# A four-layer graph network on one core: the last layer's messages with 384 radial columns and a second accumulator chunk, its frames made one layer earlier

## The chip, the core and the metric

The kernel runs on one core of a Trainium2 chip, as one program. The metric is the device time of one execution in microseconds. The kernel before takes 22,061.15 us, the median of 3 runs (22,058.3 to 22,079.04).

## The reference, cut to what matters

There are 12,500 nodes with 32 features each and 400,000 edges, sorted by target. Four layers follow each other; each sums messages over the edges into their targets, adds the result to `x` and applies a layernorm. Only the last layer's messages are changed. The 32 features are 8 scalars (kind l=0) and 8 vectors (l=1).

```python
R = relu(abs_distances[:, None] @ w1 + b1) @ w2 + b2     # 64 hidden, 384 radial values an edge
Y = spherical_harmonics(rel_vec)                         # the edge's direction
Fj = features[src]
...
# for each pair (lo, li) of output and input kinds, and each lf between |lo-li| and lo+li:
acc = acc + _NORM[i] * einsum('euv,ef,evi,ofi->euo', Rb[..., k], Yf, Fb, C)
...
out = zeros.at[dst].add(msg)
x = _layernorm(x + out)
```

If the vectors are turned into a frame of three orthogonal directions that goes with the edge (one of them along the edge), the tensor C becomes sparse: each output component (8 scalars; 8 vectors along each of three directions) is a sum over 16 inputs, weighted by radial values. That makes 32 sums of 16 products an edge. The two directions across the edge share one set of radial weights, so there are three different sets of 8 x 16 for the four kinds of output.

Layer 2 uses `edge_attr_2` to make three Gaussian weights an edge, and sums the products of these with `x[src]`.

## The kernel before, in words

**Tiling.** Edges stand 128 to a column. A step handles T = 5 columns (640 edges), a turn is G = 25 steps, a layer has NG = 25 turns, 625 steps in all. At every turn, `prepare` makes what depends on the edges alone for 25 steps (L924 for layer 2, L988 for layer 3). It is called for the next turn in the middle of the present one (`turns`, in `edge_pass`).

**A step.** GpSimd gathers the source rows with five indirect DMAs into `xg` (L338). A one-hot matrix `hot` says which of 64 nodes of a window each edge goes to; layer 3 loads it from DRAM, where layer 0 left it. TensorE multiplies the messages by it, five columns into one PSUM tile `agg` (L368), and VectorE adds `agg` into the accumulator `acc` in SBUF, at a column that a register holds (L388). Features lie on the partitions of `acc`, nodes along it.

**Layer 2** copies five steps' gathered rows into PSUM by ScalarE (L396), from a ring of three batches, makes 96 products and a count, and accumulates 97 rows. Its `prepare2` computes the Gaussians: four VectorE instructions (L930 to L944) and an exponential on ScalarE. In turn 1 it also zeroes layer 3's accumulator (L926).

**Layer 3** is made in four parts, which `run_ahead` (L403 to L428) puts in an order by hand: the products of step s, then the front and radial part of step s+1, then the reduction of step s, then the addition and the aggregation.

- `front3` (L1030): SP loads the distances into `dist` (L1037), ScalarE makes `h` (L1042); VectorE multiplies the gathered vectors by the three frame directions (`tv`, L1056, three instructions) and sums them (L1061); four small ScalarE copies fill the rest of `fa`, the 4 x 16 inputs of the four kinds (L1064 to L1069).
- `radial3` (L1072): for batches of 2, 2 and 1 columns, ScalarE copies the bias `b2r` into PSUM (L1077) and TensorE adds `h` times `wr`, 512 columns (L1082). `wr` holds the shared set of weights twice. There are three PSUM tiles for this.
- `multiply3` (L1093): VectorE multiplies these 512 values a column by `fa` into `big`, one instruction for each batch (L1097).
- `reduce3` (L1105): VectorE sums each 16 products, 2560 to 160 elements (L1109), and turns the three vector components back with three instructions (L1116); the messages are 80 wide (columns 24 to 104).

Its `prepare3` (L988) makes the frames of a turn: one load `sh` of 562.5 KB, 18 VectorE instructions (L996 to L1027) of 125 to 375 elements and a square root on ScalarE (L999).

**Node passes.** `node_pass` (L449 on) multiplies `acc` by a small matrix of weights on TensorE (`ps`, L525), transposes, adds `x_cur` and applies the layernorm. For layer 3 the weights are `wc3`, an 80 x 32 matrix of zeros and ones.

**What sets the order.** A scheduler (list scheduling over the recorded dependences) orders every engine's instructions when the program is built; pools of tiles with a fixed number of buffers set what waits for what. `work` tiles have two buffers unless said otherwise; layer 3's `agg` has one, its `xg` ring six.

Of the kernel before, what the change touches and what calls it, by code (L numbers as in the profile page):

```python
# [20 lines left out]
P = 128  # L21
F = 32
# [4 lines left out]
Q = 4  # L27
BN = 16
V = 16
EPS_LN = 1e-5  # L30
# [11 lines left out]
def kernel(  # L42
# [188 lines left out]

    wr = const.tile([P, 4, 8, 16], F32, name="wr")
    b2r = const.tile([P, 4, 8, 16], F32, name="b2r")
    wc3 = const.tile([80, F], F32, name="wc3")
    nc.vector.memset(wc3, 0.0)
    nc.sync.dma_start(wc3[0:8, 0:8], ident[0:8, 0:8])
    for f in range(3):
        nc.sync.dma_start(wc3[8 + 24 * f : 32 + 24 * f, 8:F], ident[0:24, 0:24])
    cent = const.tile([P, 4], F32, name="cent")
# [3 lines left out]
    with (  # L243
# [39 lines left out]
        for w, r in ((w2s, wr), (b2s, b2r)):  # L283
            r00 = w[:, 0:64].rearrange("h (u v) -> h u v", v=8)
            r01 = w[:, 64:128].rearrange("h (u v) -> h u v", v=8)
            r10 = w[:, 128:192].rearrange("h (u v) -> h u v", v=8)
            r11 = w[:, 192:384].rearrange("h (u v k) -> h k u v", v=8, k=3)
            nc.vector.tensor_scalar(r[:, 0, :, 0:8], r10, n1 * ca, None, op0=ALU.mult)
            nc.vector.tensor_scalar(tmp, r11[:, 2], 2.0 * n1 * c2, None, op0=ALU.mult)
            nc.vector.scalar_tensor_tensor(  # L290
                r[:, 0, :, 8:16], r11[:, 0], n1 * c0, tmp, op0=ALU.mult, op1=ALU.add
            )
            nc.vector.tensor_scalar(tmp, r11[:, 2], -n1 * c2, None, op0=ALU.mult)
            for o in (1, 2):
                nc.vector.tensor_scalar(r[:, o, :, 0:8], r11[:, 1], n1 * c1, None, op0=ALU.mult)
                nc.vector.scalar_tensor_tensor(
                    r[:, o, :, 8:16], r11[:, 0], n1 * c0, tmp, op0=ALU.mult, op1=ALU.add
                )
            nc.vector.tensor_scalar(r[:, 3, :, 0:8], r00, n0 * ca, None, op0=ALU.mult)
            nc.vector.tensor_scalar(r[:, 3, :, 8:16], r01, n0 * ca, None, op0=ALU.mult)  # L300

# [3 lines left out]

    hot_d = dram.tile([NS, P, T, W], F32, name="hot_d")

    basis_d = dram.tile([NG, 16, GT, P], F32, name="basis_d")
# [4 lines left out]
    def edge_pass(layer, pools, acc, prepare, product, chunks, xg_psum=False):  # L313
# [3 lines left out]


        io, work, ps_agg, ps_x, xgs = pools
        nch = len(chunks)  # L320
        rows = chunks[0][1] - chunks[0][0]

# [25 lines left out]
        def one_hot(i, s, begun, first):  # L348
# [13 lines left out]
            return hot  # L362

        def aggregate(prod, hot):
            agg = ps_agg.tile([rows, nch, W], F32, name="agg")
            for c, (a, b) in enumerate(chunks):
                for t in range(T):
                    nc.tensor.matmul(  # L368
                        agg[:, c, :],
                        prod[:, t, a:b],  # L370
                        hot[:, t, :],
                        start=(t == 0),
                        stop=(t == T - 1),
                    )
            return agg
# [341 lines left out]

    def sums_of(es, layer, rows, side):
        pool = es.enter_context(tc.tile_pool(name=f"acc{layer}", bufs=1, side=side))
        return pool.tile([rows, 1, N + W], F32, name=f"acc{layer}")  # L720

# [176 lines left out]

    acc3 = sums_of(ctx, 3, 80, "left")
    with ExitStack() as sums_es:  # L900
      own = sums_es.enter_context(tc.tile_pool(name="own", bufs=1)).tile([PB, NB, F], F32, name="own")
      with ExitStack() as es:
# [21 lines left out]
        def prepare2(i, first):  # L924
            if first and isinstance(i, int) and i == 1:
                nc.vector.memset(acc3, 0.0)  # L926
            u = io.tile([P, GT, 2], F32, name="u")
# [16 lines left out]
            nc.vector.tensor_reduce(gauss, d, AX.X, ALU.add)  # L944
            nc.scalar.activation(gauss, gauss, AF.Exp, scale=-0.5)
            return gauss

        def product2(gauss, i, s, xg):
            prod = prods[s % 3]
            nc.vector.tensor_tensor(  # L950
                prod[:, :, 0:96].rearrange("p t (k f) -> p t k f", f=F),
                gauss[:, s * T : (s + 1) * T, :, None].to_broadcast([P, T, 3, F]),
                xg[:, :, None, :].to_broadcast([P, T, 3, F]),
                ALU.mult,
            )
            return prod

        edge_pass(2, pools, acc2, prepare2, product2, [(0, 97)], xg_psum=True)
      node_pass(2, acc2, [wc2], own=own)
    layer2.close()  # L960

    if True:
      with ExitStack() as es:
        pools = layer_pools(es, 3, agg_bufs=1, x_bufs=0)
        io, work = pools[:2]
        ps_r = es.enter_context(tc.tile_pool(name="psr", bufs=3, space=PSUM))
        batches = [(t, min(t + 2, T)) for t in range(0, T, 2)]  # L970
        one = es.enter_context(tc.tile_pool(name="one3", bufs=1))
        dists = [one.tile([P, 3, P], F32, name=f"dist{i}") for i in range(4)]
        for d in dists:
            nc.vector.memset(d, 0.0)

        for _ in range(3):
            pr = ps_r.tile([P, 2, 512], F32, name="pr")
            for k in range(2):
                nc.tensor.matmul(
                    pr[:, k, :],  # L980
                    ident[0:64, :],
                    wr[0:64].rearrange("h o u j -> h (o u j)"),
                    start=True,
                    stop=True,
                )

        fas = []

        def prepare3(i, first):
            if not first:  # L990
                fas.clear()
            sh = io.tile([P, GT, 9], F32, name="sh")
            nc.sync.dma_start(sh, sh_t[i])
# [6 lines left out]
            nc.vector.reciprocal(nr, nr)  # L1000
            fr = io.tile([P, GT, 3, 3], F32, name="fr")
            e2, e1, q = (fr[:, :, k, :] for k in range(3))

# [22 lines left out]
            )  # L1026
            nc.vector.tensor_scalar(e2[:, :, 2:3], q[:, :, 1:2], -1.0, None, op0=ALU.mult)  # L1027
            return fr

        def front3(fr, i, s, xg):  # L1030
# [23 lines left out]
            tv = work.tile([P, T, 3, 8, 3], F32, name="tv")  # L1054
            for f in range(3):
                nc.vector.tensor_tensor(  # L1056
                    tv[:, :, f], v, frs[:, :, f, None, :].to_broadcast([P, T, 8, 3]), ALU.mult
                )

            fa = work.tile([P, T, 4, 16], F32, name="fa", bufs=3)  # L1060
            nc.vector.tensor_reduce(  # L1061
                fa[:, :, 1:4, 8:16], tv, AX.X, ALU.add
            )
            nc.scalar.copy(  # L1064
                fa[:, :, 0:4:3, 0:8], xg[:, :, None, 0:8].to_broadcast([P, T, 2, 8])
            )
            nc.scalar.copy(fa[:, :, 0, 8:16], fa[:, :, 3, 8:16])
            nc.scalar.copy(fa[:, :, 1, 0:8], fa[:, :, 2, 8:16])
# [3 lines left out]
        def radial3(st):  # L1072
            h = st[0]
            prs = []
            for a, b in batches:
                pr = ps_r.tile([P, 2, 512], F32, name="pr")
                nc.scalar.copy(  # L1077
                    pr[:, : b - a, :],
                    b2r.rearrange("p o u j -> p (o u j)")[:, None, :].to_broadcast([P, b - a, 512]),
                )  # L1080
                for k in range(b - a):
                    nc.tensor.matmul(  # L1082
                        pr[:, k, :],
                        h[64 * k : 64 * k + 64, a // 2, :],
# [8 lines left out]
        def multiply3(st, prs):  # L1093
            fa = st[2].rearrange("p t o j -> p (t o) j")
            big = work.tile([P, T * 4, 8, 16], F32, name="big")
            for (a, b), pr in zip(batches, prs):
                nc.vector.tensor_tensor(  # L1097
                    big[:, a * 4 : b * 4],
                    pr[:, : b - a, :].rearrange("p t (o u j) -> p (t o) u j", u=8, j=16),
                    fa[:, a * 4 : b * 4, None, :].to_broadcast([P, (b - a) * 4, 8, 16]),  # L1100
                    ALU.mult,
                )
            return big

        def reduce3(st, big):  # L1105
            frs = st[1]

            msg = work.tile([P, T, 104], F32, name="msg", bufs=3)
            nc.vector.tensor_reduce(  # L1109
                msg[:, :, 0:32],  # L1110
                big.rearrange("p (t o) u j -> p t (o u) j", o=4),
                AX.X,
                ALU.add,
            )
            for o, f in ((0, 2), (1, 0), (2, 1)):
                nc.vector.tensor_tensor(  # L1116
                    msg[:, :, 32 + 24 * o : 56 + 24 * o].rearrange("p t (u i) -> p t u i", i=3),
                    msg[:, :, 8 * o : 8 * o + 8, None].to_broadcast([P, T, 8, 3]),
                    frs[:, :, f, None, :].to_broadcast([P, T, 8, 3]),
                    ALU.mult,  # L1120
                )
            return msg

        edge_pass(3, pools, acc3, prepare3, (front3, radial3, multiply3, reduce3), [(24, 104)])
      node_pass(3, acc3, [wc3])

# [111 lines left out]
```

## Time and profile before

| | us |
|---|---|
| median of the runs (3) | 22,061.15 |
| the profiled execution | 22,074.03 |
| its span | 22,072.3 |
| layer 0, about | 113 to 6,220 |
| layer 1, about | 6,400 to 12,290 |
| layer 2 | 12,290 to 17,099 |
| node pass 2 | 17,099 to 17,150 |
| layer 3 | 17,150 to 22,023 |
| node pass 3 | 22,023 to 22,072 |

Busy time in the two layers that matter, from the windows of busy time:

| window | TensorE | VectorE | ScalarE | GpSimd | granted clock |
|---|---|---|---|---|---|
| layer 2, 4,809 us | 1,178.0 | 840.1 | 198.6 | 2,982.2 | 0.50 |
| layer 3, 4,873 us | 3,458.9 | 4,735.2 | 2,394.7 | 3,170.3 | 0.73 |

The mean granted clock of the whole execution is 0.592 of full speed. How to read the rows that follow: a group's row names its line, engine, operation, output and inputs with shape, then `x` and the count; behind the bar stand its busy time in us and the mean of one instruction in ns, and behind the next bar the idle time of its engine just before such instructions, with what ended it. "issue" means that the engine waited for nothing that the profile shows, "remote" a semaphore whose sender isn't seen. A row of the timeline has the start and the length in us, and in brackets the idle time before it. A row of the windows has, for each engine, the busy time and the number of instructions, then the granted clock of TensorE, the busy share of the DMA engines and GB/s.

### The profile page before, as it was taken

Reading aid. Unit: us, or ns where it says so; the run is one execution under the profiler, and the core shown is the slowest. Engines: PE = TensorE matmul, PEld = TensorE weight load, DVE = VectorE, ACT = ScalarE, POOL = GpSimd, SP = SyncE. Lnnn points to the kernel's source line nnn. Section 1 sums busy time; section 2 is a strip of 40 time slices with the busy share of each in tenths; the row PEclk is TensorE's granted clock in tenths of the full one; section 3 lists DMA queues with packets and bytes.
Section 4 is the critical chain, followed back from the end, with each engine's and each line's share of the span. In section 5 each row is a group of like instructions: output and inputs, shape, how many; then the busy total and the mean of one; then the engine's idle time right before and its main releaser. Section 6 shows DMA issues by size and latency. Waiting matters only on the chain. (4 is left out here: it accounts for less than half of the span.)

```text
span 22072.3 us, 184851 instructions
## 1 busy us (share of the span) xinstructions
PE 11780.7 (53%) x51591; PEld 9437.9 (43%) x51592; DVE 9910.1 (45%) x17560; ACT 3692.3 (17%) x8558; POOL 13971.0 (63%) x12511
## 2 busy tenths in 40 slices
PE   3444444444477777777776122222222676777776
PEld 3444444444467676666666122222222333333333
DVE  2222222222244444444444211111111999999999
ACT  0000000000011111111111000000000444444444
POOL 5444444444438888888888666666665666666665
PEclk9995555555555555555555555555555777777777
DMA  2111111111157777777777100000000222222222
GB/s 53 39 35 33 34 33 32 32 34 32 32 130 134 134 134 133 132 132 132 132 133 125 29 12 12 12 12 12 12 11 11 57 56 57 57 57 57 57 55 50
DMA packets 1970324, 1360.33 MB, mean 62 GB/s; under 512 B 1133365, under 2 KB 1713359, under 8 KB 1965888
## 3 DMA queue, kind: packets, MB, share of 16 engines
q1 hardware_dynamic: 1212955, 1126.81, 19.8%
q0 software_dynamic: 750000, 205.60, 11.3%
q10 hardware_dynamic: 6308, 15.77, 0.2%
q8 instruction: 423, 6.93, 0.1%
q14 instruction: 638, 5.23, 0.1%
HBM read 1127.48 MB, written 219.34 MB: 61 GB/s over the span
## 5 line engine op out<-in xcount | busy, mean ns | idle before, releaser
L338 POOL DMA_INDIRECT xg<-x,src_all x6250 | 6153.2, 985 | 3587.1 <-issue 2125.7
L368 PE MATMUL agg<-hot,prod 128*124 128x64 f32 (+1 forms) x18750 | 3878.3, 399 | 6857.4 <-DVE prod L663 2617.6
L368 PEld LDWEIGHTS agg<-hot,prod 128*124 128x124 f32 (+1 forms) x18750 | 3686.0, 309 | 7056.3 <-issue 6084.1
L841 POOL DMA_INDIRECT sums<-adds,tos x3125 | 4864.0, 1556 | 1238.6 <-issue 936.3
L338 POOL DMA_INDIRECT xg<-in_x_in,src_all x3125 | 2952.5, 945 | 3177.3 <-ACT xp L396 2208.4
L388 DVE TENSOR_TENSOR acc<-acc,agg 124x128 f32 (+2 forms) x1875 | 448.1, 239 | 8547.7 <-remote 6200.4
L1082 PE MATMUL pr<-wr,h 64*128 64x512 f32 x6250 | 2778.5, 917 | 772.6 <-ACT pr L1077 472.1
L806 PE MATMUL pe<-yw,bm 128*128 128x32 f32 x12500 | 2789.4, 401 | 62.3 <-DVE bm L786 53.8
L806 PEld LDWEIGHTS pe<-yw,bm 128*128 128x128 f32 x12500 | 2742.1, 333 | 70.4 <-DVE bm L786 60.3
L786 DVE SCALAR_TENSOR_TENSOR bm<-rel_p,nid,bas 128x640 f32<-128x640 f32 x1250 | 1088.1, 880 | 2966.8 <-ACT rel_p L768 2900.6
L835 PE MATMUL pm<-msg,same 128*128 128x32 f32 x6250 | 1461.0, 403 | 1537.8 <-DVE same L820 1318.6
L835 PEld LDWEIGHTS pm<-msg,same 128*128 128x128 f32 x6250 | 1380.7, 329 | 1617.8 <-issue 1427.3
L396 ACT COPY xp<-xg 128x160 f32<-128x160 f32 x1250 | 368.6, 296 | 9670.6 <-DVE prod L669 4135.4
L1097 DVE TENSOR_TENSOR big<-pr,fa 128x1024 f32<-128x1024 f32 x1875 | 1842.6, 1031 | 99.6 <-issue 43.9
L1082 PEld LDWEIGHTS pr<-wr,h 64*128 64x128 f32 x6250 | 951.0, 271 | 2033.2 <-issue 1401.6
L1109 DVE TENSOR_REDUCE msg<-big 128x160 f32<-128x2560 f32 x625 | 1753.3, 2805 | 0.0
L1077 ACT COPY pr<-b2r 128x1024 f32<-128x1024 f32 x1875 | 1594.8, 872 | 828.1 <-DVE big L1097 654.9
L368 PEld LDWEIGHTS agg<-hot,msg 128*80 128x80 f32 x6250 | 594.6, 176 | 1294.5 <-DVE acc L388 1155.4
L368 PE MATMUL agg<-hot,msg 128*80 128x64 f32 x6250 | 690.0, 268 | 641.5 <-DVE acc L388 560.4
L836 ACT COPY adds<-pm 128x160 f32<-128x160 f32 x625 | 182.6, 292 | 3194.6 <-DMA sums<-adds,tos 1691.6
L354 DVE TENSOR_TENSOR hot<-consts,rel_all 128x320 f32<-128x320 f32 x1250 | 601.8, 482 | 3.6 <-DVEq L880 3.6
L828 DVE TENSOR_REDUCE later<-dup 128x5 f32<-128x640 f32 x625 | 513.2, 821 | 21.1
(167 smaller groups left out, 6796.4 us busy)
## 6 DMA issues: line engine op xcount, KB each, us to landing
bas<-basis_d SPq DMA_DIRECT2D x625, 320.0 KB
rel<-rel_d SPq DMA_DIRECT2D x625, 320.0 KB
row<-in_src_n SPq DMA_DIRECT2D x625, 320.0 KB
hot_d<-hot SPq DMA_DIRECT2D x625, 160.0 KB
yw<-y_d SPq DMA_DIRECT2D x3125, 32.0 KB
xg<-x,src_all POOLq DMA_INDIRECT x6250
hot<-hot_d SPq DMA_DIRECT2D x625, 160.0 KB
dist<-in_ew_n SPq DMA_DIRECT2D x625, 96.0 KB
```

The costliest lines, as they stand in the source:

```text
L338: nc.gpsimd.indirect_dma_start(out=xg[:, t, :], out_offset=None, in_=x_dram[layer], in_offset=bass.IndirectOffsetOnAxis(ap=src[:, s * T + ...
L354: nc.vector.tensor_tensor(hot, iota_w[:, None, :].to_broadcast([P, T, W]), begun[1][:, s, :, None].to_broadcast([P, T, W]), ALU.is_equal,)
L368: nc.tensor.matmul(agg[:, c, :], prod[:, t, a:b], hot[:, t, :], start=(t == 0), stop=(t == T - 1),)
L786: nc.vector.scalar_tensor_tensor(bm[:, h], rel_p, ids[:, h : h + 1], bas, op0=ALU.is_equal, op1=ALU.mult)
L806: nc.tensor.matmul(pe[:, t, :], bm[:, h, t, :], yw[:, t, h * F : (h + 1) * F], start=(h == 0), stop=(h == 1),)
L828: nc.vector.tensor_reduce(later, dup, AX.X, ALU.max)
L835: nc.tensor.matmul(pm[:, t, :], same[:, t, :], msg[:, t, :], start=True, stop=True)
L841: into = nc.gpsimd.indirect_dma_start(out=sums[t], out_offset=bass.IndirectOffsetOnAxis(ap=tos[:, k, t : t + 1], axis=0), in_=adds[:, k, t ...
L1077: nc.scalar.copy(pr[:, : b - a, :], b2r.rearrange("p o u j -> p (o u j)")[:, None, :].to_broadcast([P, b - a, 512]),)
L1082: nc.tensor.matmul(pr[:, k, :], h[64 * k : 64 * k + 64, a // 2, :], wr[64 * k : 64 * k + 64].rearrange("h o u j -> h (o u j)"), start=Fals ...
L1097: nc.vector.tensor_tensor(big[:, a * 4 : b * 4], pr[:, : b - a, :].rearrange("p t (o u j) -> p (t o) u j", u=8, j=16), fa[:, a * 4 : b * 4 ...
L1109: nc.vector.tensor_reduce(msg[:, :, 0:32], big.rearrange("p (t o) u j -> p t (o u) j", o=4), AX.X, ALU.add,)
```

## The change

1. The scalar outputs' sums of 16 are no longer made for each edge. The 128 products of the fourth kind go to the aggregation as they are, as a second chunk of 128 rows; the accumulator gets 128 partitions and two chunks, and the last node pass sums each 16 rows with a second matrix of weights, `wc3s`. The reduction keeps three kinds (1920 to 120 elements), and the messages of the first chunk are 72 wide.
2. `wr` and `b2r` hold the three different sets once, 384 columns. The multiplication reads the middle set for two kinds, by a view of PSUM that overlaps itself (`by_kind`).
3. The frames are made by `frames`, called in layer 2's `prepare2`, and written to DRAM; `prepare3` loads them.
4. `tv` is made by one instruction of 360 elements, and so is the turning back.
5. The accumulator of layer 3 is allocated when layer 2's memory is free, and zeroed at the start of layer 3. Its `agg` tile is made once (AGG3 = 1) and zeroed once.

```diff
-    wr = const.tile([P, 4, 8, 16], F32, name="wr")
-    b2r = const.tile([P, 4, 8, 16], F32, name="b2r")
-    wc3 = const.tile([80, F], F32, name="wc3")
+    wr = const.tile([P, 3, 8, 16], F32, name="wr")
+    b2r = const.tile([P, 3, 8, 16], F32, name="b2r")
+    wc3 = const.tile([72, F], F32, name="wc3")
+    wc3s = const.tile([P, F], F32, name="wc3s")
...
+        if layer == 3:
+            agg_n = [0]
+            aggs = [ps_agg.tile([rows, nch, W], F32, name=f"agg{k}") for k in range(AGG3)]
+            for a in aggs:
+                nc.vector.memset(a, 0.0)
...
             for c, (a, b) in enumerate(chunks):
+                part = prod[c] if layer == 3 else prod
                 for t in range(T):
                     nc.tensor.matmul(
-                        agg[:, c, :],
-                        prod[:, t, a:b],
+                        agg[: b - a, c, :],
+                        part[:, t, a:b],
                         hot[:, t, :],
...
-    acc3 = sums_of(ctx, 3, 80, "left")
...
         def prepare2(i, first):
-            if first and isinstance(i, int) and i == 1:
-                nc.vector.memset(acc3, 0.0)
...
             nc.scalar.activation(gauss, gauss, AF.Exp, scale=-0.5)
+            if first:
+                frames(i)
             return gauss
+        def frames(i):
+            sh = io.tile([P, GT, 9], F32, name="sh", bufs=1)
             nc.sync.dma_start(sh, sh_t[i])
...
+            nc.sync.dma_start(
+                fr_d[ds(i, 1)].rearrange("a p (e k) -> (a p) e k", k=9), fr.rearrange("p e f i -> p e (f i)")
+            )
...
+      acc3 = sums_of(ctx, 3, P, "left", 2)
+        nc.vector.memset(acc3, 0.0)
...
+        def by_kind(pr):
+            return bass.AP(
+                pr.tensor,
+                pr.offset,
+                [list(pr.ap[0]), list(pr.ap[1]), [128, 2], [128, 2], [16, 8], [1, 16]],
+            )
         def prepare3(i, first):
+            fr = io.tile([P, GT, 3, 3], F32, name="fr")
+            nc.sync.dma_start(
+                fr.rearrange("p e f i -> p e (f i)"), fr_d[ds(i, 1)].rearrange("a p (e k) -> (a p) e k", k=9)
+            )
             return fr
...
-            for f in range(3):
-                nc.vector.tensor_tensor(
-                    tv[:, :, f], v, frs[:, :, f, None, :].to_broadcast([P, T, 8, 3]), ALU.mult
-                )
+            nc.vector.tensor_tensor(
+                tv,
+                v[:, :, None].to_broadcast([P, T, 3, 8, 3]),
+                frs[:, :, :, None, :].to_broadcast([P, T, 3, 8, 3]),
+                ALU.mult,
+            )
...
-                        pr[:, k, :],
+                        pr[:, k, :R3],
...
-                    pr[:, : b - a, :].rearrange("p t (o u j) -> p (t o) u j", u=8, j=16),
+                    by_kind(pr[:, :n, :]),
...
-            msg = work.tile([P, T, 104], F32, name="msg", bufs=3)
+            msg = work.tile([P, T, 96], F32, name="msg")
+            big = big.rearrange("p (t o) u j -> p t o u j", o=4)
             nc.vector.tensor_reduce(
-                msg[:, :, 0:32],
-                big.rearrange("p (t o) u j -> p t (o u) j", o=4),
-                AX.X,
-                ALU.add,
-            )
-            for o, f in ((0, 2), (1, 0), (2, 1)):
-                nc.vector.tensor_tensor(
-                    msg[:, :, 32 + 24 * o : 56 + 24 * o].rearrange("p t (u i) -> p t u i", i=3),
...
+                msg[:, :, 0:24].rearrange("p t (o u) -> p t o u", u=8), big[:, :, 0:3], AX.X, ALU.add
+            )
+            nc.vector.tensor_tensor(
+                msg[:, :, 24:96].rearrange("p t (o u i) -> p t o u i", o=3, i=3),
...
-        edge_pass(3, pools, acc3, prepare3, (front3, radial3, multiply3, reduce3), [(24, 104)])
-      node_pass(3, acc3, [wc3])
+            return msg, big[:, :, 3].rearrange("p t u j -> p t (u j)")
+        edge_pass(3, pools, acc3, prepare3, (front3, radial3, multiply3, reduce3), [(24, 96), (0, 128)])
+      node_pass(3, acc3, [wc3, wc3s])
```

## The prediction

> **What bounds the kernel now.** I read the 40 slices of the page first, because the four layers have different limits and a share of the whole span means little. The last slices are layer 3.
>
> ```profile
> DVE  2222222222244444444444211111111999999999
> ACT  0000000000011111111111000000000444444444
> POOL 5444444444438888888888666666665666666665
> PEclk9995555555555555555555555555555777777777
> ```
>
> In layer 3 (the last nine digits) VectorE is full, ScalarE half busy, GpSimd two thirds. In layer 2 (eight digits before) VectorE has next to nothing to do. The windows of busy time say it in numbers: the first row is a piece of layer 2, the second one of layer 3 (the columns are PE, weight loads, VectorE, ScalarE, GpSimd, then the granted clock).
>
> ```profile
> 12800.00:16800.00 4000.00, 977.16 (x5240) 894.84 (x5240) 688.29 (x1653) 162.33 (x545) 2493.24 (x2624) 0.50 0.08 12
> 17200.00:21900.00 4700.00, 3353.26 (x12132) 1498.81 (x12132) 4592.82 (x7706) 2325.37 (x4873) 3081.06 (x3035) 0.73 0.24 56
> ```
>
> VectorE is busy 98% of layer 3 and 17% of layer 2. The page's chain of waits covers only the closing node pass and is of no use here. So a step of layer 3 costs what VectorE spends on it. The groups by shape between 17400 and 21900 us price that:
>
> ```profile
> L1109 DVE TENSOR_REDUCE msg<-big 128x160 f32<-128x2560 f32 x581 | 1629.8, 2805 | 0.0
> L1097 DVE TENSOR_TENSOR big<-pr,fa 128x1024 f32<-128x1024 f32 x1164 | 1366.3, 1209 | 88.9 <-issue 43.9 <-remote 31.4 <-PE agg L368 7.7
> ...
> L1097 DVE TENSOR_TENSOR big<-pr,fa 128x512 f32<-128x512 f32 x582 | 392.6, 675 | 3.8 <-remote 2.5 <-PE pr L1082 1.1 <-PE agg L368 0.2
> L1116 DVE TENSOR_TENSOR msg<-msg,fr 128x120 f32<-128x120 f32 x1743 | 382.4, 268 | 0.0
> L1056 DVE TENSOR_TENSOR tv<-xg,fr 128x120 f32<-128x120 f32 x1743 | 382.2, 269 | 0.0
> ...
> L1061 DVE TENSOR_REDUCE fa<-tv 128x120 f32<-128x360 f32 x581 | 295.3, 508 | 0.0
> ...
> L388 DVE TENSOR_TENSOR acc<-acc,agg 80x64 f32 x581 | 120.4, 207 | 4.9 <-remote 1.7 <-issue 0.3
> ...
> L996 DVE TENSOR_TENSOR sq<-sh 128x375 f32<-128x375 f32 x23 | 12.3, 534 | 0.0
> L998 DVE TENSOR_REDUCE nr<-sq 128x125 f32<-128x375 f32 x23 | 12.2, 532 | 0.0
> ```
>
> One step is a 2.805 reduction, 2 x 1.209 + 0.675 of products, 3 x 0.268, 3 x 0.269, 0.508 and 0.207: 8.22 us of durations in twelve instructions. In the timeline steps follow each other every 7.32 us, so neighbours overlap by 0.90 / 12 = 0.075 us each. The only idle time of note is 89 us before the products, in some 45 stalls.
>
> **The change, part by part.** The sums start from the profiled execution, 22,074.0 us.
>
> *The steps of layer 3.* The reduction goes from 2560 to 1920 elements. The slope between the 375- and the 2560-element rows is (2805 - 532) / 2185 = 1.040 ns, so it saves 640 x 1.040 = 0.67 us. Three 120-element instructions become one of 360, twice: three cost 3 x (0.268 - 0.075) = 0.58, one costs about 0.52 (the 375-element row has 0.534) less 0.075, so 0.44; saved 2 x 0.14. The addition into acc grows from 64 to 128 elements; layer 0 does 124x128 in 0.288 us, so +0.08. The products keep their 1024 and 512 elements, and the overlapping view changes only addresses: I price that at nothing, from 0 to +0.05 us a step. Together 0.67 + 0.27 - 0.08 = 0.85 us; the step falls to 6.47, and 625 x 0.853 = **533 us** saved.
>
> *The frames leave layer 3.* They are 18 VectorE instructions a turn, from 0.26 to 0.93 us, 7.8 us of durations, 6.4 at VectorE's pace (7.8 - 18 x 0.075). All of it lies on the path: 25 x 6.4 = **160 us** saved. Their ScalarE square root goes too; the 562 KB load stays, of the frames instead of the harmonics, on SP's queue at the same place.
>
> *The frames enter layer 2.* Per frame: 18 VectorE instructions (7.8 us), a square root that now alternates with layer 2's exponential (by the built program 22 further table loads on ScalarE, 1.28 us each like the ones in the trace), a load and a store of 562 KB on SP. The scheduler puts all 25 into the first ten turns, one every nine or ten steps. What sets layer 2's pace is GpSimd, which gathers in batches of five steps and then waits for the ScalarE copy that frees its ring:
>
> ```profile
> L338 POOL DMA_INDIRECT xg<-x,src_all x2624 | 2493.2, 950 | 1501.6 <-issue 761.3 <-ACT xp L396 724.1 <-DMA xg<-x,src_all 16.1
> ```
>
> A batch takes 36.9 us, 31.2 of it gathers. VectorE has time enough, so the frame's own 7.8 us are hidden as long as it stays 17% busy; without that cover they would cost 7.8 + 2.6 us and a little more, some 13 us a frame. A frame may still delay the copy that GpSimd waits for, by its table loads and by making the products late that release it, and its dozen instructions with two SBUF inputs can lengthen gathers. The nearest row is layer 2's own turn work (three 750-element instructions and a reduction, 3.7 us, and an exponential): the turn's five batches with it take 191 us, those without 184.5, so about 6 us go through. Bounds: 0 to 13 us a frame. I take 6 because the row is like it: **+150 us** (0 to +330). On SP, behind the store that waits for the frame, stands the next load of `u`, needed a turn later: nobody waits.
>
> *The accumulator.* Its memset of 80x12564 (10.5 us) leaves layer 2; one of 128x25128 (layer 0 has 21.0 us for 124x25128) comes before the first tv of layer 3, exactly where two turns' frames stood (17,145 to 17,159). First agg waits, in both, for a first product, and VectorE already stood idle 21 us there: **+5 us** (-10 to +20).
>
> *The last node pass.* Two weights double its 32-column matmuls; eight take 0.65 us, 25 groups: 8 to 16 us, as PE is busy 30 of the pass's 49 us: **+12 us**.
>
> *PE and GpSimd in layer 3: new waits.* PE gets ten more instructions a step (128 columns of weights) and loses a quarter of the 512-column products. Two stretches show that the price of its work depends on the clock:
>
> ```profile
> 18162.00:18168.00 6.00, 3.18 (x12) 0.98 (x10) 6.00 (x11) 3.06 (x7) 4.06 (x5) 1.00 0.28 66
> 18152.00:18160.00 8.00, 7.69 (x23) 3.54 (x21) 8.00 (x14) 3.82 (x8) 5.57 (x6) 0.50 0.23 55
> ```
>
> By the timeline, a step's PE work is now 1.59 (agg) + 5.5 (pr) = 7.1 us in half-clock steps and 0.93 + 3.17 = 4.1 in full-clock ones. After: agg 3.7 and 2.1 (by columns of weights, 200 to 80, it would be 4.0 and 2.3), pr 4.2 and 2.4: **7.9 at half, 4.5 at full**, against VectorE's 6.47. At half clock PE can't keep up. Here a rule speaks: the Trainium skill, "TensorE: Matmul & The Clock Gate", Part 1, has the clock double after about 3.4 us of sustained work and fall back after an idle window as long. The trace agrees on the rise (the half-clock row, 7.69 of 8 us busy, is followed by 1.00), but the clock falls again after gaps of only 1 to 2 us. By the rule alone PE would sit at full clock, with no cost. By the row, half-clock spells go on, each putting PE 1.4 us behind in a step, about what agg and pr have as slack before the products want pr. I take 0.05 us a step.
>
> GpSimd is no longer held back by its ring. It needs 5 x 1.247 = 6.24 us a step, if no gather is lengthened (0.94 and 0.30 before each, as the first row below has it):
>
> ```profile
> 17994.50 0.94 POOL L338 DMA_INDIRECT xg<-x,src_all  x1 [0.30 <-issue]
> ...
> 18000.00 1.33 POOL L338 DMA_INDIRECT xg<-x,src_all  x1 [0.30 <-DVE fa L1061]
> ```
>
> The second began beside the msg products. The Trainium skill, "GPSIMD Engine Reference", section 1, says why: GpSimd shares its SBUF interfaces with VectorE, and contends with VectorE instructions of two SBUF inputs. By the rule every tv and msg instruction can cost a gather its whole length, 2 x 0.44 us, making 7.1 us a step; by the row 0.39 each, at most 7.0; and where the gathers' phase drifts clear of them, 6.24. Since VectorE's 6.47 lies near the low end and the two can fall into step, I take 0.05 us a step here too. Together 0.1 x 625 = **+60 us** (0 to +330).
>
> Sum: 22,074 - 533 - 160 + 150 + 5 + 12 + 60 = 21,608. The median of the runs, 22,061.2, is 13 us under the profiled time; the forecast for the median is **21,595 us** (-2.1%).
>
> **The rivals.**
>
> *GpSimd becomes the bound.* At 6.8 to 7.0 us a step, 0.23 to 0.43 more than the 6.57 forecast: +145 to +270 us, so 21,740 to 21,865. For it: the ring's wait vanishes, and lengthened gathers are in the trace. Against: one instruction in place of three locks less often.
>
> *Frames in layer 2 are free* (and PE and GpSimd cost nothing): -210, so 21,385. For it: VectorE is 83% idle there. Against: the 6 us of its own turn work. Or they cost their full 13: 21,775.
>
> *PE becomes the bound*, the case on the other side. If the clock stays at half, as it does in layer 1 with PE busy 70% of the time, a step costs 7.9 us, 1.33 over the forecast: 21,595 + 830 = 22,425, slower. It decides once a step takes more than 6.57 + 466 / 625 = 7.32 us, which between 7.9 at 0.50 and 4.5 at 1.00 is a mean granted clock under about 0.59 (0.73 now). Against it: a PE that is full at half clock was granted full clock within a few us.
>
> *The view doesn't do what it says*: if a six-dimensional overlapping read slows the products by a tenth, 0.3 us a step, 21,785.
>
> **How the numbers follow.** Forecast as summed (21,480 to 21,720): 0.60. Frames and the rest nearly free (21,360 to 21,480): 0.11. GpSimd, the view or dear frames (21,720 to 21,900): 0.21. PE bound: 0.05 slower, 0.01 about the same. Something not seen: 0.02, half of it slower. The range 21,390 to 21,850 leaves out the ends of the second and third cases and the PE case. About 0.2% is what a measurement of this kernel can tell from no change: faster 0.93, same 0.01, slower 0.06.
>
> **What would show it.** VectorE still 95% busy or more in layer 3 with a step of 6.5 us; reduction 2.14, merged instructions 0.52, acc 0.29; layer 2 longer by 150 us, all in its first half; gathers' waits mostly "issue"; granted clock 0.7 or more in layer 3. Wrong would be: VectorE idle before the products on PE's pr, or before tv on the gathers, for more than 0.3 us a step, or products longer than 1.21.

## The result and the profile after

The changed kernel takes 22,713.5 us (median of 4 runs, 22,697.0 to 22,736.2) against 22,062.4: a ratio of 1.0296, with a 95% interval of 1.0283 to 1.0309. It is slower by 651 us where 466 us less had been forecast, and lies outside the range of 21,390 to 21,850. The profiled execution took 22,720 us.

The slices of the page after, the same four rows as before:

```profile
DVE  2222222222254444444443222111116777777777
ACT  0000000000011111111110000000002333333333
POOL 5444444444358888888886666666664555555554
PEclk9995555555555555555555555555556666666666
```

The last ten digits are layer 3. VectorE was full there; now it is at seven tenths, ScalarE and GpSimd have fallen as well, and no engine is full. The row of the windows for a long piece of layer 3 says the same: VectorE 3,447 of 4,600 us, GpSimd 2,498, granted clock 0.64.

```profile
18000.00:22600.00 4600.00, 3513.99 (x15852) 2316.85 (x15851) 3446.76 (x4226) 1739.70 (x4226) 2497.58 (x2643) 0.64 0.22 50
```

The groups by shape in that stretch, VectorE alone (the last figures are its idle time before such instructions):

```profile
L1139 DVE TENSOR_TENSOR big<-pr,fa 128x1024 f32<-128x1024 f32 x1056 | 1257.7, 1221 | 812.0 <-issue 464.3 <-remote 213.4 <-PE agg L388 94.3
L1155 DVE TENSOR_REDUCE msg<-big 128x120 f32<-128x1920 f32 x529 | 1135.3, 2146 | 0.0
L1139 DVE TENSOR_TENSOR big<-pr,fa 128x512 f32<-128x512 f32 x528 | 359.8, 681 | 15.1 <-issue 6.0 <-remote 4.0 <-PE pr L1123 2.8
L1158 DVE TENSOR_TENSOR msg<-msg,fr 128x360 f32<-128x360 f32 x528 | 276.9, 524 | 0.0
L1096 DVE TENSOR_TENSOR tv<-xg,fr 128x360 f32<-128x360 f32 x528 | 276.6, 524 | 0.0
L1104 DVE TENSOR_REDUCE fa<-tv 128x120 f32<-128x360 f32 x529 | 274.2, 518 | 0.0
L408 DVE TENSOR_TENSOR acc<-acc,agg 128x128 f32 x528 | 149.4, 283 | 326.1 <-remote 297.1 <-PE pr L1123 19.5 <-issue 9.0
```

Every duration of the forecast holds: the reduction 2.146 us (2.14 forecast), the merged instructions 0.524 (0.52), the addition 0.283 (0.288), the products 1.221 (1.209). What is new stands behind the second bar: 812 + 15 + 326 = 1,153 us of idle time in 528 steps, 2.18 us a step, where before it was 98 us in 581. It stands before the two instructions that wait for TensorE: the products (for pr) and the addition (for agg).

The timeline of one such wait (start, length, instruction, idle time before):

```profile
20001.90 0.28 DVE L408 TENSOR_TENSOR acc<-acc,agg 128x128 f32 x1
...
20002.97 0.86 PE L388 MATMUL agg<-hot,msg 128*72 128x64 f32 x10
20003.52 0.94 POOL L346 DMA_INDIRECT xg<-x,src_all  x1 [0.30 <-issue]
...
20003.67 1.28 PE L388 MATMUL agg<-hot,big 128*128 128x64 f32 x10
20004.77 0.94 POOL L346 DMA_INDIRECT xg<-x,src_all  x1 [0.30 <-issue]
20006.47 1.22 DVE L1139 TENSOR_TENSOR big<-pr,fa 128x1024 f32<-128x1024 f32 x1 [4.29 <-issue]
...
20008.09 0.33 SPq L360 DMA_DIRECT2D hot<-hot_d  x1
...
20010.86 0.94 POOL L346 DMA_INDIRECT xg<-x,src_all  x1 [5.15 <-ACT fa L1105]
```

The products could start at 20002.2. They wait for the first batch of pr, which stands ahead of agg on TensorE; at 20002.97 TensorE had gone on to agg, and by 20004.95 it had done that too. VectorE went on at 20006.47. The profile has VectorE's wait instruction ahead of the products as one of 4.73 us: VectorE stood at a semaphore, not at data. SP's load of `hot`, which waits for agg, came 3.1 us after agg's end; on a chip where nothing waits (below) it comes 0.04 us after it. So a second reader of TensorE's semaphore saw it late too. GpSimd gathers one after another meanwhile, 0.30 us apart, until 20005.71; VectorE goes on 0.8 us after that, and GpSimd, whose ring is full, only at 20010.86. This repeats: in most of layer 3 GpSimd now makes ten gathers in a row (with 0.5 us in place of 0.30 between the fifth and the sixth) and then pauses some 5 us. The start of layer 3 shows it larger:

```profile
17220.95 2.34 PE L388 MATMUL agg<-hot,big 128*128 128x64 f32 x10
...
17246.98 0.95 POOL L346 DMA_INDIRECT xg<-x,src_all  x1 [0.30 <-issue]
17253.86 0.34 SPq L360 DMA_DIRECT2D hot<-hot_d  x1
17253.87 0.29 DVE L408 TENSOR_TENSOR acc<-acc,agg 128x128 f32 x1 [32.49 <-remote]
```

The first agg is done at 17223.3. GpSimd gathers without a pause until 17247.9, and at 17253.86 SP and VectorE, which wait for the same agg, are released in the same hundredth of a microsecond, 30.6 us late. At the end of the layer, with GpSimd's gathers over, the waits are gone and a step takes 6.49 us (products at 22644.61 and 22651.10).

The page before had the sign in a row that the prediction didn't read, that of the additions in all layers:

```profile
L388 DVE TENSOR_TENSOR acc<-acc,agg 124x128 f32 (+2 forms) x1875 | 448.1, 239 | 8547.7 <-remote 6200.4
```

6,200 us of waiting for a sender that isn't seen, nearly all in layers 0 and 2, where GpSimd gathers 25 times and more without a pause. In layer 3 before, VectorE's longer step held GpSimd back: in most steps it stands idle for 1.0 us after five gathers, and 98 us of VectorE's waiting were left.

```profile
18031.96 0.94 POOL L338 DMA_INDIRECT xg<-x,src_all  x1 [1.00 <-issue]
...
18039.27 0.94 POOL L338 DMA_INDIRECT xg<-x,src_all  x1 [0.99 <-issue]
```

### The profile page after: what moved, and what is told of

The parts are those of the page before. It is cut to its first block, busy times and chain, and to the rows that moved or that the text cites. A ratio compares the mean times of both kernels' runs of the same rounds, so it can differ in the third digit from the quotient of the medians.

```text
span 22718.3 us, 195279 instructions
## 1 busy us (share of the span) xinstructions
PE 12496.3 (55%) x58041; PEld 10651.0 (47%) x58042; DVE 9425.5 (41%) x15059; ACT 3386.4 (15%) x8580; POOL 13766.5 (61%) x12511
## 5 line engine op out<-in xcount | busy, mean ns | idle before, releaser
L346 POOL DMA_INDIRECT xg<-x,src_all x6250 | 5950.3, 952 | 4424.0 <-issue 1807.9
L408 DVE TENSOR_TENSOR acc<-acc,agg 124x128 f32 (+2 forms) x1875 | 496.2, 265 | 8828.4 <-remote 6584.9
L1123 PE MATMUL pr<-wr,h 64*128 64x384 f32 x6250 | 2362.8, 793 | 691.5 <-ACT pr L1118 616.3
L1123 PEld LDWEIGHTS pr<-wr,h 64*128 64x128 f32 x6250 | 1007.5, 289 | 1543.8 <-ACT pr L1118 870.4
L1118 ACT COPY pr<-b2r 128x768 f32<-128x768 f32 x1875 | 1263.1, 695 | 2100.3 <-DVE big L1139 1258.3
L1155 DVE TENSOR_REDUCE msg<-big 128x120 f32<-128x1920 f32 x625 | 1341.3, 2146 | 0.0
L388 PEld LDWEIGHTS agg<-hot,msg 128*72 128x72 f32 x6250 | 658.3, 199 | 1201.5 <-DVE acc L408 419.7
L388 PE MATMUL agg<-hot,big 128*128 128x64 f32 x6250 | 1198.2, 363 | 0.0
L388 PEld LDWEIGHTS agg<-hot,big 128*128 128x128 f32 x6250 | 1144.3, 277 | 0.0
L388 PE MATMUL agg<-hot,msg 128*72 128x64 f32 x6250 | 762.8, 293 | 635.3 <-DVE acc L408 337.9
```

The lines of the kernel that those rows point to most:

```text
L346: nc.gpsimd.indirect_dma_start(out=xg[:, t, :], out_offset=None, in_=x_dram[layer], in_offset=bass.IndirectOffsetOnAxis(ap=src[:, s * T + ...
L388: nc.tensor.matmul(agg[: b - a, c, :], part[:, t, a:b], hot[:, t, :], start=(t == 0), stop=(t == T - 1),)
L408: adds.append(nc.vector.tensor_tensor(cols, cols, agg, ALU.add))
L1118: nc.scalar.copy(pr[:, : b - a, :R3], b2r.rearrange("p o u j -> p (o u j)")[:, None, :].to_broadcast([P, b - a, R3]),)
L1123: nc.tensor.matmul(pr[:, k, :R3], h[64 * k : 64 * k + 64, a // 2, :], wr[64 * k : 64 * k + 64].rearrange("h o u j -> h (o u j)"), start=False,
L1155: nc.vector.tensor_reduce(msg[:, :, 0:24].rearrange("p t (o u) -> p t o u", u=8), big[:, :, 0:3], AX.X, ALU.add)
```

## The experiments

Two theories. **Theory 1**: TensorE's semaphores reach VectorE and SP late while GpSimd gathers without a pause; the shorter step took the pause away. **Theory 2**: TensorE itself is late, with ten more matmuls and weight loads a step at half clock. The executions came from several chips, and that turned out to matter: on some, as on the one of the measurement above, the kernel before takes 22,050 to 22,100 us; on others 18,830 to 18,860, with the same instructions. I call them chips with and without late semaphores. Chips 1 and 2 were of the first sort; 3, 9, 11, 12 (met twice) and 15 of the second; the number of the first measurement's chip is not on record. No chip was met in both ways, so that the chip decides, and not the occasion, rests on these few.

**One gather a step.** Four of five gathers of layer 3 left out:

```diff
         def gathered(s, begun):
+            if layer == 3:
+                xg1 = work.tile([P, 1, F], F32, name="xg", bufs=6)
+                nc.gpsimd.indirect_dma_start(
+                    out=xg1[:, 0, :],
...
+                )
+                return xg1.to_broadcast([P, T, F])
```

> The changed kernel, with one gather a step in layer 3 instead of five: the first column's rows are used for all five, so four fifths of layer 3's gathered data are left out, and every other instruction stays. Theory 1 (VectorE's waits for a TensorE semaphore end late while GpSimd issues gathers one after another without a pause, and the shorter step took that pause away): the waits go, a step of layer 3 takes VectorE's 6.5 us, layer 3 falls from 5,494 to about 4,100 us and the time to about 21,320 us (21,200 to 21,450). Theory 2 (TensorE itself is late: ten more instructions a step at half clock): nothing changes, 22,600 to 22,750 us.

Measured 18,155.6 us, but the kernel before took 18,855.6 beside it. The comparison with 22,720 was void: another chip.

**A fifth of the second chunk's matmuls:**

```diff
-                for t in range(T):
+                cols = range(1) if c else range(T)
+                for t in cols:
...
-                        stop=(t == T - 1),
+                        stop=(t == cols[-1]),
```

> The changed kernel, with one matmul of five in the second chunk of the aggregation: four columns' scalars are left out of the sums; the addition keeps its 128x128. TensorE loses eight of its twenty added instructions and weight loads a step, some 1.9 us at half clock. Theory 1 (late semaphores beside unbroken gathers): VectorE still waits before the products and the addition, 22,300 to 22,750 us. Theory 2 (TensorE is late): a step comes near 6.6 us, 21,400 to 21,700 us.

Measured 18,173.2 us beside 18,855.6, on a chip without late semaphores. Taking eight matmuls a step away gains nothing there against the changed kernel as it is (18,169.4, below).

**The old reduction of four kinds:**

```diff
-            msg = work.tile([P, T, 96], F32, name="msg")
+            msg = work.tile([P, T, 104], F32, name="msg")
...
-                msg[:, :, 0:24].rearrange("p t (o u) -> p t o u", u=8), big[:, :, 0:3], AX.X, ALU.add
+                msg[:, :, 0:32].rearrange("p t (o u) -> p t o u", u=8), big, AX.X, ALU.add
...
```

> The changed kernel, with the old reduction of 2560 elements to 160 (the fourth kind's sums are made and not used), so VectorE works 0.67 us more a step, 7.15 us. Theory 1: GpSimd gets a pause of 0.9 us a step, the waits become rare and the kernel gets faster by added work: 21,950 to 22,400 us. Theory 2: TensorE's 7.9 us at half clock still bound the step, so 22,700 us or a little more. If neither holds and VectorE's work simply adds up: 23,100 us.

Measured 18,582.7 us beside 18,855.6. VectorE has no gap at all in layer 3 (2,999.84 of 3,000 us), with TensorE and its twenty added instructions unchanged:

```profile
15000.00:18000.00 3000.00, 2480.08 (x12659) 1671.65 (x12658) 2999.84 (x3374) 1388.05 (x3373) 2089.99 (x2110) 0.74 0.26 62
```

**The frames alone** (the kernel before with `frames` in `prepare2`, a store, and a load in `prepare3`, as in the change):

> The kernel before, with its frames made in layer 2 and loaded in layer 3, nothing else changed. Layer 2 longer by 30 to 40 us (the changed kernel's trace), layer 3 shorter by 25 x 6.4 = 160 us by both theories, so 21,930 to 21,970 us; by theory 1 it could be up to 100 us more, because 18 VectorE instructions a turn no longer give GpSimd a pause.

Measured 18,689.2 us beside 18,855.6.

**The changed kernel again**, to see whether the chip or the change makes the difference:

> The changed kernel once more, unaltered. In the four runs before this one the kernel before took 18,856 us where it took 22,061 at first, with the same instructions; VectorE's waits with a sender that isn't seen were gone from all layers. If the chip decides (a chip on which TensorE's semaphores reach VectorE late beside gathers, and one on which they don't), then where the kernel before takes about 18,856 us the changed one takes 18,856 - 533 - 160 + 40 + 12 + 10 = 18,225 us (18,130 to 18,330); where it takes about 22,061 us the changed one takes 22,700 us again. If the change itself makes the late waits, it is slower by some 600 us on either.

Measured 22,728.9 us beside 22,077.7, ratio 1.0291 (1.0274 to 1.0308): a chip with late semaphores, and the first result once more.

> The changed kernel, unaltered. If the kernel before takes about 18,856 us here (no late semaphores): 18,225 us (18,130 to 18,330). If it takes about 22,070: 22,720 us.

Measured 18,186.5 us beside 18,841.2.

> The changed kernel, unaltered, timed. Where the kernel before takes 18,850 us: 18,187 us again (18,170 to 18,200), 0.965 of it. Where it takes 22,070 us: 22,720 us, 1.03 of it.

Measured 18,169.4 us (4 runs) beside 18,838.2 (7 runs), ratio 0.9643 (0.9627 to 0.9659). On a chip without late semaphores the same program is faster by 669 us. Its groups on VectorE in layer 3, the two that wait for TensorE:

```profile
L1139 DVE TENSOR_TENSOR big<-pr,fa 128x1024 f32<-128x1024 f32 x1216 | 1431.6, 1218 | 1.8 <-issue 1.7
...
L408 DVE TENSOR_TENSOR acc<-acc,agg 128x128 f32 x606 | 170.4, 281 | 0.6 <-PE agg L388 0.3
```

2.4 us of idle time in place of 1,153. TensorE's agg is seen at once (it ends at 16005.62):

```profile
16004.34 1.28 PE L388 MATMUL agg<-hot,big 128*128 128x64 f32 x10
...
16005.66 0.36 SPq L360 DMA_DIRECT2D hot<-hot_d  x1
```

A step in its timeline takes 6.44 us (one addition starts at 16003.31, the next at 16009.75), and TensorE's granted clock is 0.77:

```profile
14000.00:18000.00 4000.00, 3407.88 (x18457) 2313.24 (x18457) 3971.32 (x4933) 2013.76 (x4903) 3021.98 (x3057) 0.77 0.28 67
```

The page's row of all additions has there, in place of 8,828 us of idle time (6,585 of it "remote") in the changed kernel's first profile:

```profile
L408 DVE TENSOR_TENSOR acc<-acc,agg 124x128 f32 (+2 forms) x1875 | 495.0, 264 | 2993.7 <-PE agg L388 2988.6
```

Now the releaser is seen: TensorE, when it is done. From its first to its last addition layer 0 takes 3,914 us here and 6,101 on the chip of the first profile, layer 2 3,913 and 4,718, layer 3 4,025 and 5,413: nearly all of the 4,550 us between the two executions. On such a chip theory 2 falls with this: the same TensorE work, with no wait.

**Plain loads**: layer 3's gathers replaced by five loads a step on SP's queue, so that GpSimd does nothing there and the bytes stay (by the page's queues in more packets, 144 a load where a gather has 32):

```diff
+            if layer == 3:
+                for t in range(T):
+                    nc.sync.dma_start(xg[:, t, :], x_dram[layer][P * (s * T + t) % 12288 : P * (s * T + t) % 12288 + P, :])
+                return xg
```

> The changed kernel, with layer 3's gathers replaced by five plain loads a step on SP's queue, of the same size and packets (128 rows of 128 bytes each), from fixed rows: the gathered data are left out, GpSimd does nothing in layer 3, the DMA traffic stays. Where the kernel before takes 22,070 us: if GpSimd's own work makes the semaphores late, 21,330 us like one gather a step; if the small packets and their semaphore increments do, 22,000 to 22,800 us. SP issues eight transfers a step, some 5 of 6.5 us, so 100 us more are possible on either. Where the kernel before takes 18,850 us: 18,190 us, up to 18,300.

Measured 18,160.6 us beside 18,845.4: a chip without late semaphores. It shows only that GpSimd costs the changed kernel next to nothing there: 14 us on the one chip that ran both (e17 below, 18,155.9, and 18,169.4 with the gathers).

**One gather a step, on a chip with late semaphores:**

> The changed kernel with one gather a step in layer 3 (four fifths of that layer's gathered data left out). Where the kernel before takes 22,070 us: about 21,330 us (21,250 to 21,450) if the gathers make TensorE's semaphores late there, above 22,000 us if they are late whatever is gathered. Where the kernel before takes 18,850 us: 18,160 us as three times before.

Measured 21,254.0 us (one execution) beside 22,046.2. This is the run that theory 1 needed. VectorE in layer 3, window and groups:

```profile
17300.00:21100.00 3800.00, 3278.31 (x17672) 2235.02 (x17670) 3797.16 (x4710) 1937.88 (x4709) 555.36 (x589) 0.77 0.21 58
```

```profile
L1148 DVE TENSOR_TENSOR big<-pr,fa 128x1024 f32<-128x1024 f32 x1178 | 1387.1, 1219 | 2.6 <-issue 2.6
...
L417 DVE TENSOR_TENSOR acc<-acc,agg 128x128 f32 x588 | 165.3, 281 | 0.2
```

No wait is left, VectorE is busy 3,797 of 3,800 us, and a step takes 3,800 / 589 = 6.45 us. TensorE does all its work here, so theory 2 falls on this sort of chip too. From first to last addition layer 3 takes 4,026 us, where without late semaphores it took 4,025. In the same execution layers 0 and 2, whose gathers are untouched, keep their late waits:

```profile
DVE acc L417 <- remote: 6092.8, 432, 28.6
```

So the waits go with the gathers, layer by layer, on one chip and in one run.

The traces also hold the times at which semaphores were raised, which the rows above do not print. Counting a TensorE update as late when it stands more than 0.5 us behind the end of the last TensorE instruction that raises this semaphore:

| kernel and layer | GpSimd's indirect DMAs in a row | updates recorded | late | median of the late, us |
|---|---|---|---|---|
| one gather (e18), layer 3 | 1 | 2,432 | 2 | 1.1 |
| before, layer 3 | 5 | 1,816 | 426 | 0.9 |
| changed, layer 3 | 10 | 2,324 | 1,231 | 2.5 |
| before, layer 2 | 25 to 50 | 539 | 248 | 10.8 |
| before, layer 0 | 25 | 676 | 238 | 12.8 |
| before, layer 1 (scatters) | over 3,000 | 991 | 0 | |
| changed, layer 3, other chip (e16) | over 3,000 | 2,492 | 0 | |

Three things follow. The raising itself is late, and in these rows it is the later, the more gathers GpSimd makes in a row. It concerns TensorE's semaphore: in the changed kernel's first trace 1,739 of 4,843 TensorE updates are late, but 31 of 8,835 of VectorE's and 2 of 4,912 of ScalarE's. And an unbroken row of indirect DMAs is not enough: layer 1 scatters without a pause on the same chip (1.56 us each, 0.30 us apart, where a gather takes 0.94) and no update is late. On these chips the record has gaps, 8,835 updates for 13,854 VectorE instructions that raise one (13,830 on the other chip), so the counts are of what was recorded.

**Repeats.** The remaining runs were meant for a chip with late semaphores and fell on others. They confirm the numbers above, and leave open what they were for.

| run | us | the kernel before beside it |
|---|---|---|
| one gather (e7) | 18,153.7 | 18,841.2 |
| one gather (e10, 2 runs) | 18,167.8 | 18,845.4 |
| four kinds reduced (e8) | 18,593.4 | 18,841.2 |
| four kinds reduced (e12, 2 runs) | 18,589.2 | 18,845.4 |
| frames alone (e9) | 18,706.1 | 18,841.2 |
| frames alone (e14) | 18,703.4 | 18,847.2 |
| plain loads (e13) | 18,167.3 | 18,847.2 |
| plain loads (e15, 4 runs) | 18,170.1 | 18,849.1 |
| plain loads (e17, 2 runs) | 18,155.9 | 18,838.2 |

What was expected of them, in the order of the table:

> The changed kernel with one gather a step in layer 3 instead of five (four fifths of that layer's gathered data left out), to be run where semaphores are late. Theory 1 (they are late only beside unbroken gathers): layer 3 takes 625 x 6.5 us plus its start, and the time falls from 22,720 to about 21,330 us (21,250 to 21,450). If that chip's TensorE semaphores are late whatever GpSimd does, or DMA traffic at large makes them late: above 22,000 us. Where the kernel before takes 18,856 us: 18,155 us as in the first run.

> The changed kernel with one gather a step in layer 3 (four fifths of that layer's gathered data left out), timed, to be run where the kernel before takes about 22,070 us. Theory 1 (TensorE's semaphores arrive late there while GpSimd gathers without a pause): layer 3's waits go, its step is VectorE's 6.5 us, 21,330 us (21,250 to 21,450) against 22,720. Theory 3 (on that chip they arrive late whatever GpSimd does): above 22,000 us. Where the kernel before takes 18,850 us: 18,155 us.

> The changed kernel with the old reduction of 2560 elements (0.67 us more VectorE work a step), to be run where semaphores are late. Theory 1: a pause of 0.9 us a step comes back to GpSimd, the waits become rarer, and the kernel gets faster by added work: 22,000 to 22,450 us against 22,720. If the waits have nothing to do with GpSimd's pauses: 22,720 us or more, up to 23,100. Where the kernel before takes 18,856 us: 18,583 us as in the first run.

> The changed kernel with the old reduction of 2560 elements (0.67 us more VectorE work a step), timed. Where the kernel before takes 22,070 us, theory 1: GpSimd has a pause of 0.9 us a step again, the waits become rarer, and added work makes it faster, 22,000 to 22,450 us against 22,720. Theory 3: 22,720 to 23,100 us. Where the kernel before takes 18,850 us: 18,590 us.

> The kernel before with its frames made in layer 2 and nothing else changed, to be run where semaphores are late. Layer 3 keeps its step of 7.32 us and GpSimd its pause of 1 us: 22,070 - 160 + 40 = 21,950 us; up to 22,050 if the frames' time was itself a pause that kept waits away. Where the kernel before takes 18,856 us: 18,690 us as in the first run.

> The kernel before with its frames made in layer 2 and nothing else changed. On the chip on which the kernel before takes 22,070 us, GpSimd keeps its pause of 1 us a step: 21,950 us (21,900 to 22,050), faster than both kernels there. Where the kernel before takes 18,850 us: 18,700 us.

> The changed kernel with layer 3's gathers replaced by five plain loads a step on SP's queue (the gathered data are left out, GpSimd does nothing in layer 3, the DMA traffic stays). It is meant for the chip on which the kernel before takes 22,070 us: there, if GpSimd's own issuing of gathers makes TensorE's semaphores late, layer 3's step is 6.5 us and the time about 21,330 us (21,250 to 21,450); if the traffic of small packets does, 22,000 to 22,800 us. Where the kernel before takes 18,850 us: 18,160 us as before.

> The changed kernel with layer 3's gathers replaced by five plain loads a step on SP's queue (the gathered data are left out). Where the kernel before takes 22,070 us: about 21,330 us (21,250 to 21,450) if GpSimd's own issuing of gathers makes TensorE's semaphores late, 22,000 to 22,800 us if the traffic of small packets does. Where the kernel before takes 18,850 us: 18,160 us as twice before.

> The changed kernel with layer 3's gathers replaced by five plain loads a step on SP's queue (the gathered data are left out). Where the kernel before takes 22,070 us: about 21,330 us (21,250 to 21,450) if GpSimd's own issuing of gathers makes TensorE's semaphores late, 22,000 to 22,800 us if the traffic of small packets does. Where the kernel before takes 18,850 us: 18,165 us as before.

Open, then, because these kernels did not run on a chip with late semaphores: whether GpSimd's own issuing or the packets of its gathers delay TensorE's semaphores (layer 1 shows only that scatters, issued more slowly, do not), whether 0.9 us of pause a step would be enough there, and whether the frames alone (ratio about 0.992 elsewhere) are faster than both kernels there. Nor was it tested whether the recording of the profile, which misses a third of VectorE's updates in the changed kernel's first trace, has a part in it. Where semaphores are in time, the changed kernel itself is the fastest of those that compute the whole layer.

## Why the prediction was wrong, by its steps

**The step that failed** is the one on GpSimd: "GpSimd is no longer held back by its ring ... I take 0.05 us a step here too". It priced GpSimd's missing pause by the length of gathers beside VectorE, and put what the others suffer while GpSimd has no pause at nothing. That term was 2.18 us a step: VectorE's idle time before the products, which the prediction had named as a sign of being wrong above 0.3 us, and before the addition. The answer stood in the trace: VectorE's "some 45 stalls", named and left as they were, and the 6,200 us of "remote" in the row shown above. On the chip of the measurement that makes 625 x 2.18 = 1,363 us. No rival had this mechanism: GpSimd as the bound was the nearest in cause, at a tenth to a fifth of the price, and the one on the slower side was TensorE at half clock.

The sum nearly closes. Without late semaphores the change is worth 669 us; on the other chip 1,363 us of waits come in and the 98 us of before go out: 669 - 1,363 + 98 = -596, against -651 measured. The 55 us that remain are not fully accounted for: the start of layer 3 is longer (32.5 us of idle time before its first addition, 21.5 before), and layer 2 is 29 us longer by the trace, of which the 669 us already hold what the frames cost elsewhere.

**The steps of layer 3** were right: 6.47 us forecast; 6.44, 6.49 and 6.45 us where nothing waits. The reduction alone is 18,593.4 - 18,186.5 = 407 us on one chip (0.666 x 625 = 416 forecast). The view costs little: 1.218 and 0.681 us for the products against 1.204 and 0.669 in the frames-alone kernel, 0.04 us a step, within the 0 to 0.05 that the forecast allowed.

**The frames** cost little in layer 2. Frames alone gain 135 to 166 us on chips without late semaphores; if they leave layer 3 for the 160 us forecast (the runs show only the difference), layer 2 pays about 10 us there, not 150. The term was mis-sized: I took layer 2's own turn work as the nearest row. Why a frame costs so much less was not tested; two differences are that the frames lie apart, on average one every ten steps, and that on the chip of that trace layer 2 was waiting for late semaphores most of the time. On the chip with late semaphores layer 2 grew by 29 us (17,098 to 17,127 us at its last addition).

**The last node pass**: 48.7 us before, from the last addition to the end, and 51.3 after; +3 us for a forecast of 12.

**The accumulator**: its memset took 21.0 us, ahead of the first tv of layer 3, as forecast.

**TensorE**: where semaphores are in time it kept pace, as in the windows row of e16 above; 0.05 us a step had been set aside for half-clock spells, and the wait is nil. The granted clock was 0.77 (1,870 of those 4,000 us at half), so half-clock spells did go on, as my row had it; what was wrong was their price. The clock gate's rule of the Trainium skill ("TensorE: Matmul & The Clock Gate", Part 1), taken alone, had the cost right, but for a full clock that was not granted.

**The gathers** did lengthen as the Trainium skill ("GPSIMD Engine Reference", section 1) lets one expect:

```profile
L346 POOL DMA_INDIRECT xg<-x,src_all x3057 | 3022.0, 989 | 985.0 <-issue 797.3 <-DMA xg<-x,src_all 79.3 <-DMA x<-x_cur 53.5
```

Those of this stretch that begin beside a tv or msg instruction (two SBUF inputs) take 1.146 us, 604 in all, and beside the products, the reductions and the addition 0.944. That is 0.2 us each, 0.2 us a step. The section names the contention and no size; the prediction's "whole length", 0.44 us each, was its own bound. And nearly all of it was hidden: plain loads in the gathers' place save 14 us.

On a chip without late semaphores the forecast of 466 us would have been too low, its cautious terms all erring the same way: with the measured ones the sum reads 466 + 140 (frames) + 60 (TensorE and GpSimd) + 9 (node pass) = 675, against 669 measured, and 655 in the single pair of e6.

## What to carry to other kernels

Before shortening an engine's step, ask which engine that step was holding back, and what the others suffer when it is not held back. An idle time that the profile can't give a sender ("remote", or "issue" with the producer long done) is a quantity of its own: look up where in the span it is large, what runs there, and whether the change makes that the rule elsewhere. And a gain that lies in another engine's pauses may depend on the chip: measure on more than one.

## What the runs showed of the hardware

On some chips a semaphore that TensorE raises is raised, and seen by VectorE and SP, late while GpSimd issues gathers back to back: in layer 3 most of VectorE's waits of over 1 us, beside runs of ten gathers, were 1.5 to 5.4 us, and the one at the layer's start 30.6 us. On others the same program shows none of it. For the kernel before the difference is 22,060 against 18,840 us. VectorE's and ScalarE's semaphores were hardly ever late (31 of 8,835 and 2 of 4,912), and TensorE's were in time beside one gather a step and beside layer 1's scatters.

A gather that begins beside a VectorE instruction of 360 elements with two SBUF inputs takes 1.146 us, otherwise 0.944.

VectorE with a reduction of 2146 ns, two merged instructions of 524 ns and an addition of 283 ns can be kept busy 3,797 of 3,800 us when nothing else is late.
